# Splitting the first expert of a mixture-of-experts layer: its rows from the last batch get a slot of their own, and gathers go ahead of sums

## The chip, the core and the metric

The kernel runs on one core of a Trainium2 chip. The core has a matrix engine (TensorE, PE in the profile, with its weight loads as PEld), a vector engine (VectorE, DVE), an activation engine (ScalarE, ACT), a general engine (GpSimd, POOL) and a queue that only issues transfers (SyncE, SP). Each engine works through its own list of instructions in order and waits where an input isn't there yet. Transfers issued by SP or POOL run beside them on 16 DMA engines.

The metric is the device time of one execution in microseconds, as the median of several. The profile is that of one such execution.

## The reference

One decoder layer over 16 batches of 256 tokens, width 256, all in float32:

```python
x = ln(x + recurrent(x))                   # gated scan with 16 states
x = ln(x + cross_attention(ctx, x))        # 8 heads of 128; keys: 77 context rows and the 256 tokens
x = ln(x + experts(x))
```

The change is in the last line. `experts` scores every token against 8 experts, keeps the two best with softmax weights, and lets an expert take the first 512 tokens that chose it, in order of the tokens; later ones are dropped:

```python
ones = (weights > 0)
cap_ones = where(cumsum(ones, axis=0) <= expert_capacity, ones, 0)
inter = relu(einsum('ech,eih->eci', tokens, first_linear))     # 256 -> 512
out = einsum('eci,ehi->ech', inter, second_linear) * vals      # 512 -> 256
final = zeros.at[index].add(out)                               # the two experts of a token add up
```

So a token's place in an expert depends on all tokens before it, and the last batch can still bring rows to every expert.

## The kernel before, in words

**Batches.** A loop runs over 16 x 8 pairs of batch and head, `(b, h)`, in the source from L709. For each pair it computes keys and queries (`head_kq`), the softmax, the transposed probabilities and the output, staggered over three pairs. To the pairs hang lists of other steps (`steps`, filled by `at(b, h, f, ...)`): the recurrent part of the next batches, and the last part of the batch before. For batch b-1 these are `project` (heads 2 and 3 of batch b), `turn_tokens` (head 5), `score_experts` and `choose` (head 6), `dispatch` and `settle` (head 7). The last batch has no pairs after it, so its steps follow the loop one after the other (L722 to L728).

**Routing.** `turn_tokens` transposes 256 tokens on PE (px, L532), `score_experts` multiplies by the experts' embeddings (pl, L541), `choose` picks two experts in some twenty small DVE instructions, `dispatch` counts with two small products on PE (pc, L608 and L609) how many tokens each expert already has, which `carry` keeps from batch to batch, and works out for each token the rows it goes to (sidx, L637). Four scatters on POOL (L640, 128 rows of 262 numbers each) then write the tokens into `xg`, a table in DRAM with 512 rows for each expert. Beside its 256 values a row carries the two weights, the token's number, its first expert and its two places. `settle` writes the layer's result for tokens that no expert takes.

**Experts.** After the loop, expert by expert:

- `Rows(e)` loads the 512 rows from `xg` (SP, L747) and works out on DVE from their last columns, in 13 small instructions (L751 to L778), the weight of a row, where the token's other row is (`at`), and where the sum goes (`to`);
- `turn_rows` transposes the rows on PE (L790) and copies them out with DVE (L792) and ACT (L794);
- `first_product` (L803, ReLU on ACT at L810) and `second_product` (L818, scaled on ACT at L825, stored to the table `oe_d` by SP at L828);
- `finish` gathers on POOL, four times 128 rows, what the token's earlier expert gave (L837), adds it and the token on DVE (L850, L852), normalizes (L855 to L859, the power -0.5 on POOL at L129, L863 on DVE), and scatters the finished tokens on POOL (L864). A token with two experts is finished by the later one.

In the source the order is: first product of e, rows and transposes of e+1, second product of e, finish of e, weights of e+2. Weights of expert 0 are loaded two batches before the loop ends.

**What sets the order.** The source only says what depends on what. When the program is built, a planner goes through the instructions with its own estimates of times and puts on each engine what is ready, the earliest in the source first. So an instruction can stand on its engine ahead of others that come before it in the source, and after that the order is fixed: on the chip each engine keeps to it and waits where it must. The planner also waits with a buffer until all uses of what lay there before are over. The buffers of the attention (`work`) are given up as a whole before the expert buffers (`e2`) take their place. In PSUM there are eight banks: two under the tag `mm`, one each under `pk`, `pq`, `pa`, `po`, two under `s`. Before the change the first product uses `mm`, as routing does, and the second one `pa` and `po`.

Of the kernel before, what the change touches and what calls it, by code (L numbers as in the profile page):

```python
# [18 lines left out]
P = 128  # L19
# [19 lines left out]
def decoder_layer(  # L39
# [47 lines left out]
    xg = dram.tile([E * CAP, DX], F32, tag="xg", name="xg")  # L87

    oe_d = dram.tile([E * CAP, D], F32, tag="oe", name="oe")
# [13 lines left out]
    ebase = cpool.tile([P, GT, E], F32, tag="ebase", name="ebase")  # L103
    for e in range(E):
        G.memset(rev[:, :, e : e + 1], float(E - e))
        G.memset(ebase[:, :, e : e + 1], float(e * CAP))
# [54 lines left out]
    w2pool = ctx.enter_context(tc.tile_pool(name="wC", bufs=1))  # L161
    work = ExitStack()
    wpool = work.enter_context(tc.tile_pool(name="wB", bufs=1))
    aw = work.enter_context(tc.tile_pool(name="aw", bufs=1))
    a2 = work.enter_context(tc.tile_pool(name="a2", bufs=2))
# [20 lines left out]
    def load_xT(pr):  # L186

        xTs[pr] = b1.tile([P, DC, PT], F32, tag="xT", name=f"xT{pr}")
        nc.sync.dma_start(xTs[pr], xT[:, pr * PT : (pr + 1) * PT].rearrange("(c p) t -> p c t", p=P))

    def load_x(b):
        xts[b] = xpool.tile([P, 2, D], F32, tag="xt", bufs=3, name=f"xt{b}")
        nc.sync.dma_start(xts[b], x_in[b * S : (b + 1) * S, :].rearrange("(i p) d -> p i d", p=P))
# [61 lines left out]
    def clear(i):  # L255

        xg_z = xg.rearrange("(i p r) d -> i p (r d)", p=P, r=2)
        for j in range(2 * i, 2 * i + 2):
            nc.sync.dma_start(xg_z[j], zero)
# [12 lines left out]
    def rec_in(pr, c):  # L272

        if c == 0:
            hss[pr] = b1.tile([P, NI, PT], F32, tag="hs", name=f"hs{pr}")
# [17 lines left out]
    def rec_state(pr):  # L293
# [5 lines left out]
        dec = b1.tile([NST, PT], F32, tag="dec", name=f"dec{pr}")  # L299
        A.activation(dec, px[0:NST], AF.Exp, bias=xpb[0:NST])  # L300
        A.activation(dec, dec, AF.Exp, scale=-1.0)
        bs = b1.tile([NST, PT], F32, tag="bs", name=f"bs{pr}")
        A.activation(bs, px[32 : 32 + NST], AF.Tanh, bias=xpbh[32 : 32 + NST], scale=0.5)
        zb = b1.tile([NST, PT], F32, tag="zb", name=f"zb{pr}")
# [297 lines left out]
    def dispatch(b):  # L602
# [12 lines left out]
        V.tensor_copy(carry, base[:, GT, :])  # L615
        cum = t3("cum", b)
# [7 lines left out]
        V.tensor_tensor(place, cum, ebase, ALU.add)  # L624
# [13 lines left out]
        for t in range(GT):  # L638
            for c in range(2):
                dma = G.indirect_dma_start(  # L640
                    out=xg[:, :],
                    out_offset=bass.IndirectOffsetOnAxis(ap=sidx[:, t, c : c + 1], axis=0),
                    in_=xs[b][:, t, :],
                    in_offset=None,
                    bounds_check=E * CAP - 1,
                    oob_is_err=False,
                )
                apart("xg", dma)
# [8 lines left out]
    for h in range(H):  # L657
        at(0, h, clear, h)
    for b in range(B):
        nb = b + 1  # L660
        new_pair = nb % PB == 0 and nb < B
        if b > 0:
            at(b, 2, project, b - 1, 0)
            at(b, 3, project, b - 1, 1)
            at(b, 5, turn_tokens, b - 1)
            at(b, 6, score_experts, b - 1)
            at(b, 6, choose, b - 1)
            at(b, 7, dispatch, b - 1)
            at(b, 7, settle, b - 1)
# [38 lines left out]
    heads = [(b, h) for b in range(B) for h in range(H)]  # L708
    for i in range(len(heads) + 2):  # L709
        if i < len(heads):  # L710
            head_kq(*heads[i])
            for f, args in steps[heads[i]]:
                f(*args)
        if i >= 2:
            head_out(*heads[i - 2])
        if i < len(heads):
            head_softmax(*heads[i])
        if 1 <= i <= len(heads):
            head_turn(*heads[i - 1])
        if i == len(heads) - 2 * H:  # L720
            load_expert(0, w2pool)
    project(B - 1, 0)  # L722
    project(B - 1, 1)
    turn_tokens(B - 1)
    score_experts(B - 1)
    choose(B - 1)
    dispatch(B - 1)
    settle(B - 1)  # L728
    work.close()
# [4 lines left out]
    e2 = ctx.enter_context(tc.tile_pool(name="e2", bufs=2))  # L734
    e1 = ctx.enter_context(tc.tile_pool(name="e1", bufs=1))
    es = ctx.enter_context(tc.tile_pool(name="es", bufs=4))
    load_expert(1, e2)

    def narrow(tag, e, dtype=F32):
        return es.tile([P, NS], dtype, tag=tag, name=f"{tag}{e}")  # L740

    class Rows:


        def __init__(self, e):
            self.x = x = e2.tile([P, NS, DX], F32, tag="xe", bufs=3, name=f"xe{e}")
            nc.sync.dma_start(x, xg[e * CAP : (e + 1) * CAP, :].rearrange("(s p) d -> p s d", p=P))  # L747
# [5 lines left out]
            V.scalar_tensor_tensor(dw1, first, float(E - e), dw, ALU.is_equal, ALU.mult)  # L753
# [6 lines left out]
            V.scalar_tensor_tensor(d1, first, float(E - e), d, ALU.is_equal, ALU.mult)  # L760
# [4 lines left out]
            V.scalar_tensor_tensor(gone, other, float(e * CAP) + 0.5, other, ALU.is_lt, ALU.mult)  # L765
# [6 lines left out]
            V.tensor_scalar(late, other, float(e * CAP) + 0.5, float(OOB), ALU.is_gt, ALU.mult)  # L772
# [7 lines left out]
    rows = {0: Rows(0)}  # L780

    xets = {}

    def turn_rows(e):
        x = rows[e].x
        xet = e2.tile([P, DC, CAP], F32, tag="xet", name=f"xet{e}")
        for k in range(DC):
            pt = bank(f"pe{e}_{k}", "pk" if k == 0 else "pq", 1)
            for s in range(NS):
                T.transpose(pt[:, s * P : (s + 1) * P], x[:, s, k * P : (k + 1) * P], ident)  # L790
            if k == 0:
                V.tensor_copy(xet[:, k, :], pt)  # L792
            else:
                A.copy(xet[:, k, :], pt)  # L794
        xets[e] = xet

    def first_product(e):
        xet = xets.pop(e)
        it = e2.tile([P, NF, CAP], F32, tag="it", name=f"it{e}")
        for f in range(NF):  # L800
            pi = bank(f"pi{e}_{f}")
            for k in range(DC):
                T.matmul(  # L803
                    pi,
                    lhsT=w1_s[e][:, k, f * P : (f + 1) * P],
                    rhs=xet[:, k, :],
# [3 lines left out]
            A.activation(it[:, f, :], pi, AF.Relu)  # L810
        return it

    def second_product(e, it):
        y = e2.tile([P, NS, D], F32, tag="ye", name=f"ye{e}")
        for s in range(NS):
            po = bank(f"pf{e}_{s}", "pa" if s % 2 == 0 else "po", 1)
            for f in range(NF):
# [3 lines left out]
                    rhs=w2_s[e][:, f, :],  # L821
# [4 lines left out]
            if s % 2 == 1 and e + 1 < E:  # L826
                r0 = e * CAP + (s - 1) * P
                nc.sync.dma_start(oe_d[r0 : r0 + 2 * P, :].rearrange("(i p) d -> p i d", p=P), y[:, s - 1 : s + 1, :])  # L828
        return y

    def finish(e, y):
        R = rows.pop(e)
        g = None
        if e > 0:
            g = e2.tile([P, NS, D], F32, tag="ge", name=f"ge{e}")
            for s in range(NS):
                G.indirect_dma_start(  # L837
                    out=g[:, s, :],
                    out_offset=None,
                    in_=oe_d[0 : e * CAP, :],  # L840
                    in_offset=bass.IndirectOffsetOnAxis(ap=R.at[:, s : s + 1], axis=0),
                )
# [3 lines left out]
        for a, z in [(0, 2), (2, 4)] if e + 1 < E else [(0, 2), (2, 3), (3, 4)]:  # L846
# [14 lines left out]
            for s in range(a, z):  # L861
# [10 lines left out]
                apart(f"out{e}", dma)  # L872

    turn_rows(0)
    for e in range(E):
        it = first_product(e)
        if e + 1 < E:
            rows[e + 1] = Rows(e + 1)
            turn_rows(e + 1)
        finish(e, second_product(e, it))  # L880
        if e + 2 < E:
            load_expert(e + 2, e2)
# [50 lines left out]
```

## Time and profile before

| what | us |
|---|---|
| median of three runs | 1240.26 (1239.01 to 1243.56) |
| profiled execution, its own time | 1242.35 |
| span of its instructions | 1240.7 |
| busy: PE / DVE / ACT / POOL | 1178.6 / 720.4 / 487.3 / 269.7 |
| mean granted clock of PE | 0.978 of full speed |
| moved by DMA | 59.74 MB |

PE is busy for 95% of the span. This says little about the end of the program, where batches turn into experts; there one has to look at stretches. The lines shown below come from four views. The table by stretches gives busy times of the engines. The timeline has one instruction, or several equal ones, in a line: start, duration, engine, line of the source, operation, output and inputs by name, sizes, count, and in brackets how long the engine had been idle and what ended that. SPq is SP's queue, and its line is the issue of a transfer, not its end. A time given as idle "<-issue" is one for which the profile shows no cause.

### The profile page before, as it was taken

The page shows a single profiled execution, that of the slowest core. Times are in us where ns is not written, and L with a number is a line of the kernel's source. Part 1 is how long each engine was busy: PE and PEld are TensorE (multiplying, and loading weights), DVE is VectorE, ACT ScalarE, POOL GpSimd, SP SyncE. Part 2 cuts the span into 40 slices and gives each one's busy share as a digit, 9 for nine tenths or more (in the row PEclk, how much of TensorE's full clock was granted, in tenths as well). Part 3 has the DMA queues.
Part 4 walks back from the last instruction along what each step waited for, and adds up shares of the span by engine and source line. Part 5 has one row for each costly group of instructions (what it writes and reads, how often), then busy time and mean ns, then how long its engine had stood idle before and what let it go on. Part 6 is the DMA issues. An engine that isn't in the chain of part 4 may idle for free.

```text
span 1240.7 us, 15148 instructions
## 1 busy us (share of the span) xinstructions
PE 1178.6 (95%) x4964; PEld 836.8 (67%) x4964; DVE 720.4 (58%) x2094; ACT 487.3 (39%) x1263; POOL 269.7 (22%) x495
## 2 busy tenths in 40 slices
PE   7799999999999999999999999999999999759993
PEld 3356777677776777677767776777677777636662
DVE  6535654675568455855585547664866454525554
ACT  3134434453344343534453435343534344213331
POOL 3300021122112211131113111211112111216655
PEclk9899999999999999999999999999999999869997
DMA  8630100010001000010001000000000000036751
GB/s 271 231 131 0 37 18 28 9 54 17 29 9 50 18 21 9 25 37 8 16 20 37 4 19 21 19 12 19 2 12 12 19 4 9 24 116 151 187 160 61
DMA packets 42737, 59.74 MB, mean 48 GB/s; under 512 B 7769, under 2 KB 30726, under 8 KB 42658
## 3 DMA queue, kind: packets, MB, share of 16 engines
q1 hardware_dynamic: 35986, 49.54, 12.4%
q0 software_dynamic: 5952, 9.21, 3.3%
q8 instruction: 39, 0.64, 0.2%
q14 instruction: 40, 0.33, 0.1%
q10 hardware_dynamic: 720, 0.01, 0.0%
HBM read 36.02 MB, written 29.98 MB: 53 GB/s over the span
## 4 chain that ended last, share of the span: by engine, by line
PE 76%; DVE 9%; issue 6%; POOL 5%; DMA 3%; ACT 1%; POOLq 0%; SPq 0%; DVEq 0%; ACTq 0%
PE po L481 11%; PE pk L430 10%; PE s L445 10%; PE pw L499 9%; PE pq L435 8%; PE pv L410 8%; PE ph L278 5%; PE pa L468 4%; PE pvc L362 3%; PE px L298 2%; PE pb L468 2%; DMA ge<-oe,at 2%; PE pl L541 1%; POOL out L864 1%; POOL re L129 1%
## 5 line engine op out<-in xcount | busy, mean ns | idle before, releaser
L447 DVE TENSOR_REDUCE nm<-s 128x2 f32<-128x666 f32 x128 | 108.4, 847 | 144.9 <-PE s L445 144.7
L481 PE MATMUL po<-ptt,v 128*128 128x256 f32 (+1 forms) x768 | 189.7, 381 | 2.4 <-DVE ptt L470 2.4
L481 PEld LDWEIGHTS po<-ptt,v 128*128 128x128 f32 (+1 forms) x768 | 143.5, 190 | 57.3 <-issue 33.1
L430 PE MATMUL pk<-kvt,wkv_s 128*128 128x333 f32 x512 | 165.1, 444 | 0.0
L445 PE MATMUL s<-kt,qt 128*128 128x333 f32 x512 | 164.4, 442 | 0.0
L489 ACT ACTIVATE ot<-po,bkv_s 128x256 f32<-128x256 f32 x128 | 60.8, 475 | 234.3 <-PE po L481 232.9
L451 ACT ACTIVATE p<-s,nm 128x333 f32<-128x333 f32 x256 | 135.3, 535 | 37.9 <-DVE nm L447 28.7
L435 PE MATMUL pq<-kvt,wq_s 128*128 128x256 f32 x512 | 131.2, 378 | 0.0
L410 PE MATMUL pv<-wkv_s,kvt 128*128 128x512 f32 x256 | 121.6, 599 | 0.0
L445 PEld LDWEIGHTS s<-kt,qt 128*128 128x128 f32 x512 | 96.5, 189 | 31.3 <-ACT qt L437 0.5
L435 PEld LDWEIGHTS pq<-kvt,wq_s 128*128 128x128 f32 x512 | 96.7, 189 | 30.5 <-issue 0.5
L499 PE MATMUL pw<-wo_s,ot 128*128 128x256 f32 x512 | 116.3, 379 | 0.1
L471 ACT COPY ptt<-pb 77x256 f32<-77x256 f32 x128 | 47.1, 368 | 173.0 <-PE pb L468 170.3
L499 PEld LDWEIGHTS pw<-wo_s,ot 128*128 128x128 f32 x512 | 96.9, 190 | 13.6 <-ACT ot L489 0.5
L430 PEld LDWEIGHTS pk<-kvt,wkv_s 128*128 128x128 f32 x512 | 87.6, 191 | 23.0
L456 DVE TENSOR_SCALAR pn<-p,rs 128x333 f32<-128x333 f32 x256 | 93.2, 398 | 4.2
L640 POOL DMA_INDIRECT xg<-xs,sidx x64 | 67.5, 1055 | 100.1 <-DVE sidx L637 85.4
L470 DVE COPY ptt<-pa 128x512 f32<-128x512 f32 x128 | 87.4, 683 | 0.9 <-issue 0.6
L468 PEld LDWEIGHTS pa<-ident,pn 128*128 128x128 f32 x512 | 63.6, 141 | 34.8 <-DVE pn L456 7.1
L510 POOL TENSOR_TENSOR xb<-xs,bo_s 128x256 f32<-128x256 f32 x32 | 21.2, 683 | 283.2 <-DVE yb L512 283.2
L468 PE MATMUL pa<-ident,pn 128*128 128x128 f32 x512 | 78.5, 274 | 2.4 <-DVE pn L456 2.4
L287 DVE SCALAR_TENSOR_TENSOR cv<-hp,cw,cv 128x512 f32<-128x512 f32 x96 | 71.3, 748 | 2.0
(164 smaller groups left out, 1569.0 us busy)
## 6 DMA issues: line engine op xcount, KB each, us to landing
v<-vc SPq DMA_DIRECT2D x16, 308.0 KB
vc<-vc SPq DMA_DIRECT2D x9, 512.0 KB
xg<-zero SPq DMA_DIRECT2D x16, 262.0 KB
xe<-xg SPq DMA_DIRECT2D x8, 524.0 KB
xT<-in_xT SPq DMA_DIRECT2D x8, 512.0 KB
xt<-in_x_in SPq DMA_DIRECT2D x16, 256.0 KB
w<-in_w1T SPq DMA_DIRECT2D x8, 512.0 KB
w<-in_w2T SPq DMA_DIRECT2D x8, 512.0 KB
```

What stands on the lines that cost most here:

```text
L287: V.scalar_tensor_tensor(cv, hp[:, :, k : k + S], cw[:, c, k : k + 1], cv, ALU.mult, ALU.add)
L410: T.matmul(pv, lhsT=kvts[b][:, k, jc * P : (jc + 1) * P], rhs=wkv_s[:, k, INNER + f0 : INNER + f0 + 512], start=(k == 0), stop=(k == DC - 1),)
L430: T.matmul(pk[:, 0:J], lhsT=wkv_s[:, k, f], rhs=kvt[:, k, :], start=(k == 0), stop=(k == DC - 1))
L435: T.matmul(pq[:, 0:S], lhsT=wq_s[:, k, f], rhs=kvt[:, k, 0:S], start=(k == 0), stop=(k == DC - 1))
L445: T.matmul(s[:, ic, 0:J], lhsT=qt[:, ic * P : (ic + 1) * P], rhs=kt, start=True, stop=True)
L447: V.tensor_reduce(nm, s[:, :, 0:J], AX.X, ALU.max, negate=True)
L451: A.activation(p[:, ic, :], s[:, ic, 0:J], AF.Exp, bias=nm[:, ic : ic + 1], accum_out=sm[:, ic : ic + 1])
L456: V.tensor_scalar(pn[:, ic, :], p[:, ic, :], rs[:, ic : ic + 1], None, ALU.mult)
L468: T.transpose(dst[0:jn, c0 : c0 + P], pn[:, ic, j0 : j0 + jn], ident)
L470: V.tensor_copy(ptt[:, 0:2, :], pt01.rearrange("p (j i) -> p j i", j=2))
L481: T.matmul(po[:, 0:S], lhsT=vs[b][0:jn, jc, h * DH : (h + 1) * DH], rhs=ptt[0:jn, jc, :], start=(jc == 0), stop=(jc == 2),)
L499: T.matmul(pws[b][:, i * D : (i + 1) * D], lhsT=ot[:, h, i * P : (i + 1) * P], rhs=wo_s[:, h, :], start=(h == 0), stop=(h == H - 1),)
```

## The change

Expert 0 is split into two slots. Slot 0 holds the rows that the first fifteen batches sent it, slot 1 those of the last batch; slots 2 to 8 are experts 1 to 7. To this end:

- `xg` and `oe_d` get 256 rows more. Expert 0 keeps rows 0 to 511, slot 1 has rows 512 to 767, the other experts follow (`FIRST`). For the last batch `ebase_last` shifts expert 0's places so that they start at row 512 whatever the count.
- Batch 14's steps `turn_tokens` to `dispatch` move one head earlier (`early`), and `Rows(0)` is written ahead of the last pair of the loop. `turn_rows(0)` is written behind the last batch's `settle`.
- The recurrent part's buffers go to the other side of SBUF and are given up two batches before the end of the loop. Expert buffers that slot 0 needs (`e0`, `es`) take their place.
- The first product uses the banks of `s`, `pa` and `po`, the second one those of `mm`. Slot 1 has two tiles of 128 rows where others have four; both products and the transposes of it are half as wide.
- The gathers of slot e+1 are written right behind the second product of slot e, ahead of `finish(e)`. Weights of experts 1 and 2 are loaded together. The final scatters of all slots are declared free of conflicts with each other.

The core of the diff:

```diff
+    FIRST = [0] + [e * CAP + S for e in range(1, E)]
+    xg = dram.tile([E * CAP + S, DX], F32, tag="xg", name="xg")
+    oe_d = dram.tile([E * CAP + S, D], F32, tag="oe", name="oe")
...
+        if b == B - 2:
+            V.tensor_copy(ebase_last, ebase)
+            for t in range(GT):
+                V.tensor_scalar(
+                    ebase_last[:, t, 0:1], carry[:, 0:1], -1.0, float(CAP), ALU.mult, ALU.add
+                )
...
+    at(1, 0, clear, H)
...
         if b > 0:
+            early = int(b == B - 1)
             at(b, 2, project, b - 1, 0)
             at(b, 3, project, b - 1, 1)
-            at(b, 5, turn_tokens, b - 1)
-            at(b, 6, score_experts, b - 1)
-            at(b, 6, choose, b - 1)
-            at(b, 7, dispatch, b - 1)
+            at(b, 5 - early, turn_tokens, b - 1)
+            at(b, 6 - early, score_experts, b - 1)
+            at(b, 6 - early, choose, b - 1)
+            at(b, 7 - early, dispatch, b - 1)
             at(b, 7, settle, b - 1)
...
+    LAST = E
+    SLOTS = [(0, 0, NS), (0, CAP, GT)] + [(e, FIRST[e], NS) for e in range(1, E)]
...
     def first_product(e):
-        it = e2.tile([P, NF, CAP], F32, tag="it", name=f"it{e}")
+        it = e0.tile([P, NF, CAP], F32, tag="it", name=f"it{e}")
         for f in range(NF):
-            pi = bank(f"pi{e}_{f}")
+            if f == 0:
+                two = ps.tile([P, 2, 512], F32, tag="s", bufs=1, name=f"pi{e}")
+            pi = two[:, f, :] if f < 2 else bank(f"pi{e}_{f}", "pa" if f == 2 else "po", 1)
...
-            po = bank(f"pf{e}_{s}", "pa" if s % 2 == 0 else "po", 1)
+            po = bank(f"pf{e}_{s}")
...
+    def gather(e):
+
+        R = rows[e]
+        gs[e] = e2.tile([P, NS, D], F32, tag="ge", name=f"ge{e}")
+        for s in range(R.n):
+            G.indirect_dma_start(
+                out=gs[e][:, s, :],
+                out_offset=None,
+                in_=oe_d[0 : SLOTS[e][1], :],
+                in_offset=bass.IndirectOffsetOnAxis(ap=R.at[:, s : s + 1], axis=0),
+            )
...
-                apart(f"out{e}", dma)
+                apart("out", dma)
...
     for i in range(len(heads) + 2):
+        if i == len(heads) - 2 * H:
+            rec.close()
+            open_early()
+        if i == len(heads) - 1:
+            rows[0] = Rows(0)
...
     dispatch(B - 1)
     settle(B - 1)
+
     turn_rows(0)
+    work.close()
+    e2 = ctx.enter_context(tc.tile_pool(name="e2", bufs=2))
+    load_expert(1, e2)
+    load_expert(2, e2)
+    for e in range(LAST + 1):
         it = first_product(e)
-        if e + 1 < E:
+        if e < LAST:
             rows[e + 1] = Rows(e + 1)
             turn_rows(e + 1)
-        finish(e, second_product(e, it))
-        if e + 2 < E:
-            load_expert(e + 2, e2)
+        y = second_product(e, it)
+        if e < LAST:
+            gather(e + 1)
+        finish(e, y)
+        if 2 <= e < E - 1:
+            load_expert(e + 1, e2)
```

## The prediction

> **What bounds the kernel now.** I read the windows of 10 us first, then the timeline where TensorE (PE) stops, then GpSimd (POOL) alone through the experts, and last the tail. Columns of the windows: stretch, its length, busy us and instructions of PE, weight load, DVE, ACT and POOL, then granted clock, DMA share, GB/s.
>
> ```profile
> 1060.00:1070.00 10.00, 10.00 (x55) 8.57 (x54) 5.92 (x26) 4.20 (x13) 4.03 (x4) 1.00 0.03 7
> 1070.00:1080.00 10.00, 6.13 (x26) 4.34 (x24) 3.02 (x9) 0.47 (x1) 2.50 (x7) 0.87 0.01 2
> 1080.00:1090.00 10.00, 2.88 (x12) 2.71 (x12) 5.02 (x34) 0.20 (x1) 1.55 (x2) 0.50 0.73 232
> 1090.00:1100.00 10.00, 0.48 (x3) 0.51 (x4) 0.51 (x7) 0.00 (x0) 2.92 (x4) 0.50 0.42 118
> 1100.00:1110.00 10.00, 10.00 (x23) 4.80 (x22) 3.48 (x35) 2.38 (x4) 0.00 (x0) 0.76 0.16 52
> ```
>
> PE is full before 1070 and after 1100. Between lies a hole, in which batch 15 is routed step after step:
>
> ```profile
> 1078.29 1.23 PE L532 MATMUL px<-ident,xs 128*128 128x128 f32 x4 [3.25 <-DVE xs L143]
> 1085.72 0.58 PE L608 MATMUL pc<-on,tri 128*128 128x16 f32 x2 [3.55 <-DVE on L599]
> 1092.86 0.98 POOL L640 DMA_INDIRECT xg<-xs,sidx  x1 [0.30 <-issue]
> 1095.03 1.47 SPq L747 DMA_DIRECT2D xe<-xg  x3
> 1099.49 0.17 DVE L751 TENSOR_TENSOR dw<-xe 128x4 f32<-128x4 f32 x1 [10.76 <-DMA xe<-xg]
> 1101.39 8.80 PE L803 MATMUL pi<-xet,w 128*128 128x512 f32 x16
> ```
>
> The last projection ends at 1075.05, rows land at 1099.49: 24.4 us in which PE has 1.23 (px) + 1.88 (pl) + 1.17 (pc) of work, at half clock. The next limit is POOL, here one turn (gathers of one expert to those of the next):
>
> ```profile
> 1157.74 0.99 POOL L837 DMA_INDIRECT ge<-oe,at  x1 [0.30 <-issue]
> 1159.04 1.14 POOL L837 DMA_INDIRECT ge<-oe,at  x1 [0.30 <-issue]
> 1160.47 0.95 POOL L837 DMA_INDIRECT ge<-oe,at  x1 [0.30 <-issue]
> 1161.73 1.16 POOL L837 DMA_INDIRECT ge<-oe,at  x1 [0.30 <-issue]
> 1165.69 0.76 POOL L129 TENSOR_TENSOR re<-ve,nhalf 128x2 f32<-128x2 f32 x1 [2.79 <-DVE ve L859]
> 1170.03 0.72 POOL L129 TENSOR_TENSOR re<-ve,nhalf 128x2 f32<-128x2 f32 x1 [0.49 <-DVE ve L859]
> 1174.12 0.99 POOL L837 DMA_INDIRECT ge<-oe,at  x1 [0.30 <-issue]
> ```
>
> A turn takes 1174.12-1157.74 = 16.38 us; PE starts an expert every 14.65 (1147.64 to 1162.29). So POOL falls behind, and the tail pays: PE's last product ends at 1220.43, and only then POOL gathers for expert 7.
>
> ```profile
> 1220.43 0.47 ACT L825 ACTIVATE ye<-pf,we 128x256 f32<-128x256 f32 x1 [1.25 <-PE pf L818]
> 1223.13 0.99 POOL L837 DMA_INDIRECT ge<-oe,at  x1 [0.30 <-issue]
> 1229.00 0.76 POOL L129 TENSOR_TENSOR re<-ve,nhalf 128x2 f32<-128x2 f32 x1 [1.09 <-DVE ve L859]
> ```
>
> Tail: 1240.7-1220.43 = 20.3 us, of which 11.7 follow the power at 1229.00.
>
> **Step 1, routing batch 14 one head earlier.** No instruction is added; 4 scatters (xg) move with it. In the trace its xs are final at 1042.6 (L143), px ran at 1049.3, its scatters from 1063.53 to 1068.47. One head is 5.9 us there (pk at 1041.8, 47.3, 52.8, 58.8), so px comes near 1044, scatters end near 1062.6, and SP issues the load of expert 0's rows 1.2 us later (as 1093.84 to 1095.03), 1063.8. It lands near 1068.3, taking the 4.46 us of 1095.03 to 1099.49, in which three loads shared the engines. That load is moved past nothing on SP: after 1044.5 SP issues nothing until 1080.46. POOL is idle there. DVE then has the 13 small Rows instructions (1.2 us, 1099.49 to 1100.64), and it is in order: standing ahead of head 7's softmax they hold it until the rows land. From both sides: 0 (DVE sat idle 6.84 us before 1075.07) to 1068.3-1063.85 = 4.5. I take 0, since batch 14's other steps stood well in this loop. Three more DVE instructions (0.5 us), a ninth clear (262 KB in batch 1, DMA nearly idle): 0, hidden under PE's full row.
>
> **Step 2, expert 0 in the hole.** Its work on PE is 8 transposes (0.8), 7.03 (L803 warm), 6.84 (L818): 14.7 us, from rows, weights and banks (pk, pq, s, pa, po) free before 1075. Room is 24.4-4.3 = 20 us. In the source it stands behind the routing, but the order on an engine is a planner's, which pulls ready work ahead: batch 14's output, written in head 7, ran on POOL at 1043.55, in head 4. I take it that it does so here. Routing may then wait behind a matmul pair (0.86) at each of px, pl, pc: up to 2.6 us, against 2.1 won where px, pl, pc run at full clock (half of 4.3): net 0. The worst order, px behind all of expert 0, costs 13.3 (1091.6 for 1078.3). DVE gets one copy more (0.69), which fits into its 0.84 wait for POOL at 1077.
>
> y of expert 0 lies over the attention's buffers and waits for the last output's landing, as the weights did at 1082.75; its first use is near 1086. Its scatters (POOL, 8.2 us) follow batch 15's, after 1093.84, when POOL sat idle 22.6 us: hidden; without that cover they would delay slot 1's gathers by 8.
>
> **Step 3, the extra slot.** Same scatters, so its load still goes at 1095.03, half as large and without xe0 before it: at best 1097.3 (a 256 KB store took 2.3: issued 1080.46, SP's wait for it over at 1082.75), at worst 1099.49. I take 1098.2. With Rows (1.2) and a half copy (0.35) product 1 starts at 1099.8. PE then does: slot 1, 16 x 0.215 + 16 x 0.214 = 6.86; the turn for slot 2, 0.77; slots 2 to 7, 6 x 14.65 = 87.9; slot 8, 7.03 + 6.84 = 13.87. Sum 109.4. Slot 1 and its transposes are new: 7.3 us on the path. It also adds a 256 KB store and POOL work: 2 gathers at 1.28 (nothing joins there, so each fetches row 0), a power with its wait 1.5, 2 scatters 2.34, 6.4 us in all. POOL does this near 1105 to 1114, when it has nothing else but expert 0's leftover, so I cost it at nothing; if expert 0's scatters slip behind it, slot 2's sums start late by up to 6, which the 1.05 us that POOL then gains per turn takes back over six turns.
>
> **The clock.** The row: PE stopped at 1075.05, the clock halved by 1077.5, after 2.4 us, and came back at 1104.8, 5.3 after 1099.49; the first product took 8.80 for 7.03. The Trainium skill (TensorE: Matmul & The Clock Gate, "Part 1: The HAM clock gate") wants an idle window of about 3.4 us to cool and about 3.4 busy to warm. It speaks against the change: expert 0 ends near 1093.5, a second hole of 5 us is left, PE cools again, and the warm-up is paid at 1099.8 as before. By the rule 3.4 x 0.5 = 1.7 is lost, by the row 1.77. I take the row, and 0.7 for stalls such as that from 1130.85 to 1131.38: PE ends at 1099.8+109.4+1.8+0.7 = 1211.7, **8.7 us earlier**.
>
> **Step 4, gathers ahead of sums.** Each slot's four gathers go on POOL past the power and four scatters of the slot before. A turn loses the 2.79 wait: 16.38-2.79 = 13.6 us of POOL, below 14.65, so PE leads. But each gather now asks for a store just issued. [...]the store above took 2.3, the loaded row load 4.5. Queued behind the waiting gather are POOL's power and scatters of the slot before, and DVE's L863 waits for them. Before, 14 us lay between store and gather.
> Take PE's end of a slot as T. Gather first: y at T+0.5, landed T+2.8[...], gathers to T+8, sums' output to T+16.4, which is T'+1.8 of the next slot; no growth from slot to slot. Last slot: DVE sums at T+4.2 at the latest, power at T+4.5, end T+16.2. Power first (planner finds the store not landed): the last power at T-0.8, end T+10.9. Midway, and by no nearer row: **13.5**, against 20.3: 6.8 us.
>
> **Sum.** 1211.7+13.5 = 1225.2 for the span of 1240.7: 15.5 less. The profiled execution took 1242.35, 1.65 around its span and 2.1 over the median of 1240.26; taken off the median: **1224.8**.
>
> **Rivals.** A: as above. PE's end is at best 1206.9 (routing 2.1 sooner, rows 0.9 sooner, a clock that stays full 1.8), at worst 1213.5 (rows 1.3 later, routing 0.5); with tails of 10.9 to 16.2 and less 0.4: 1217 to 1229. Chance 0.62.
> B: the gathers' order changes nothing, POOL keeps its turn. For: POOL's order is the planner's too. Against: the chain waits on ge in each turn. Slot 2 ends at 1124; its power at 1124.2, then 6 turns as 1133.27 to 1229.00 (95.7), then 11.7: 1231.6, less 0.4 for the median: 1231. Chance 0.14.
> C: the planner keeps source order, expert 0 starts after pc (1086.7), and its second product comes behind slot 1's transposes: 1098.2 + 0.4 + 6.84 + 109.4 + 0.7 = 1215.5 (PE is warm by then), + 13.5 = 1229.0: 1228.6 on the median. For: px to pc stand earlier in the source. Chance 0.10.
> D: routing is held behind expert 0's matmuls, by 2 to 13.3 us: 1226 to 1236. Chance 0.09.
> E, slower: POOL as bound. If the wait for the store (w) adds to POOL's 13.6 each turn, and isn't hidden in PE's time, w = 4.5 makes 18.1; the first such gather is at 1109.2+4.5, the seventh 108.6 later, 1222.3, then 13.6 and 11.7: 1247.6. The end is 1216.1 + 7w, so it decides from w = 3.5, and from 4.4 it is slower by over 0.5%. Against: the store goes at PE's time, so a late POOL finds it landed. Chance 0.05.
>
> 0.5% (6.2 us) is about what a measurement of this kernel tells from no change. Below 1234: A, B, C and most of D: faster 0.92. Same, D's end and a mild E: 0.05. Slower 0.03. The range 1218 to 1234 leaves out D's end, E and a little below A.
>
> **What would show it.** Right: L803's first rows before 1085; px, pl, pc at clock 1.00; the rows' load still near 1095; PE's end near 1212; no DVE wait on ge; the tail 11 to 16. Wrong: pc later than 1088, a DVE wait on xe before 1070, POOL waiting over 5 us ahead of L837 in each turn, or turns of over 15 us.

## The result and the profile after

The changed kernel takes 1230.76 us (median of four runs, 1230.44 to 1232.08), the kernel before beside it 1241.54 (four runs, 1239.01 to 1243.56): ratio 0.9916, 95% interval [0.9894, 0.9938]. A second set on another chip gave 0.9896 [0.9871, 0.9921], or 13.3 us. The forecast was 1224.8 with a range of 1218 to 1234: the time lies in the range, but of 15.5 us forecast some 10.8 came. By spans it is 1240.7 to 1230.4, 10.3 us, and 5.2 us of the sum are missing.

The same stretches of 10 us as before, now of the changed kernel (stretch, length, busy us and instructions of PE, weight load, DVE, ACT, POOL, granted clock, DMA share, GB/s):

```profile
1060.00:1070.00 10.00, 7.04 (x34) 5.54 (x32) 3.47 (x18) 4.14 (x13) 2.81 (x3) 1.00 0.25 60
1070.00:1080.00 10.00, 9.37 (x38) 7.77 (x39) 1.56 (x8) 0.84 (x2) 0.00 (x0) 0.83 0.01 2
1080.00:1090.00 10.00, 8.92 (x35) 4.71 (x34) 6.23 (x27) 2.04 (x5) 2.92 (x7) 1.00 0.25 71
1090.00:1100.00 10.00, 9.11 (x40) 6.82 (x38) 5.47 (x27) 2.93 (x6) 4.76 (x5) 1.00 0.59 197
1100.00:1110.00 10.00, 7.51 (x33) 6.23 (x34) 6.58 (x48) 2.49 (x6) 5.89 (x7) 0.83 0.75 199
```

The hole between 1080 and 1100 is filled, at full clock. But before the change PE worked almost without a break until 1075.05, and now it has only 7.04 us in 1060 to 1070, and a clock of 0.83 in the row after. The timeline of the changed kernel shows why:

```profile
1064.63 0.37 SPq L743 DMA_DIRECT2D xe<-xg  x1
...
1065.58 1.46 PE L484 MATMUL po<-ptt,v 128*128 128x256 f32 x6
...
1069.04 0.17 DVE L748 TENSOR_TENSOR dw<-xe 128x4 f32<-128x4 f32 x1 [3.76 <-DMA xe<-xg]
...
1070.18 0.69 DVE L459 TENSOR_SCALAR pn<-p,rs 128x333 f32<-128x333 f32 x2
1070.63 0.84 PE L471 MATMUL pa<-ident,pn 128*128 128x128 f32 x4 [3.59 <-DVE pn L459]
...
1080.73 0.69 DVE L515 TENSOR_TENSOR yb<-pw,xb 128x512 f32<-128x512 f32 x1 [8.52 <-PE pw L502]
```

The same two places of the kernel before:

```profile
1065.60 1.46 PE L481 MATMUL po<-ptt,v 128*128 128x256 f32 x6
...
1075.07 0.69 DVE L512 TENSOR_TENSOR yb<-pw,xb 128x512 f32<-128x512 f32 x1 [6.84 <-PE pw L499]
```

DVE stands 3.76 us at slot 0's first Rows instruction, until the rows have landed. Behind it in DVE's order is the last head's softmax (L459), and PE waits for that (3.59 us). Just ahead of it PE is level in both profiles (po at 1065.58 and 1065.60). Batch 15's output yb starts at 1080.73, where it started at 1075.07. So the hold costs 5.66 us: the wait, and 1.7 us because PE then runs at half clock from 1071.7 to 1075.1, and some 0.4 that were not taken apart.

Then slot 0's work and the routing of batch 15, interleaved on PE, and slot 1's rows:

```profile
1084.41 0.87 PE L535 MATMUL px<-ident,xs 128*128 128x128 f32 x4 [0.35 <-DVE xs L146]
1085.12 1.02 PE L798 MATMUL pi<-xet,w 128*128 128x512 f32 x2
1086.98 3.68 PE L798 MATMUL pi<-xet,w 128*128 128x512 f32 x8
1090.67 0.36 PE L611 MATMUL pc<-on,tri 128*128 128x16 f32 x2
1092.05 7.07 PE L814 MATMUL pf<-w,it 128*128 128x256 f32 x32
1099.55 0.88 SPq L743 DMA_DIRECT2D xe<-xg  x2
1102.28 0.16 DVE L748 TENSOR_TENSOR dw<-xe 128x2 f32<-128x2 f32 x1 [1.37 <-DMA xe<-xg]
1103.52 4.86 PE L798 MATMUL pi<-xet,w 128*128 128x256 f32 x16 [0.18 <-DVE xet L785]
```

From yb to the issue of the rows' load it is 18.8 us (before: 1075.07 to 1095.03, 20.0), with the whole of expert 0 in between. Last, the tail, with ACT's last scaled product (ye) and the end of POOL's order:

```profile
1205.16 0.75 POOL L132 TENSOR_TENSOR re<-ve,nhalf 128x2 f32<-128x2 f32 x1 [1.03 <-DVE ve L859]
...
1210.90 1.03 POOL L864 DMA_INDIRECT out<-oe,to  x1 [0.74 <-DVE oe L863]
1212.23 0.99 POOL L834 DMA_INDIRECT ge<-oe,at  x1 [0.30 <-issue]
...
1216.07 0.95 POOL L834 DMA_INDIRECT ge<-oe,at  x1 [0.30 <-issue]
1216.47 0.47 ACT L821 ACTIVATE ye<-pf,we 128x256 f32<-128x256 f32 x1 [1.25 <-PE pf L814]
1217.32 1.01 POOL L864 DMA_INDIRECT out<-oe,to  x1 [0.30 <-issue]
1218.36 0.73 POOL L132 TENSOR_TENSOR re<-ve,nhalf 128x2 f32<-128x2 f32 x1
```

The last slot's gathers stand ahead of only one scatter of slot 7. For the gathers of slots 3 to 7 POOL's order is still the old one: power, two scatters, power, two scatters of the slot before, then the four gathers. PE's part ends with ye at 1216.47 (before 1220.43), the last slot's first power comes at 1218.36 (before 1229.00), and from there it is 12.0 us to the end (before 11.7). DVE's wait for ge fell from 20.6 to 10.2 us in all.

### The profile page after: what moved, and what is told of

Same layout as the page of the kernel before. It is cut to its first block, busy times and chain, and to the rows that moved or that the text cites. A ratio compares the mean times of both kernels' runs of the same rounds, so it can differ in the third digit from the quotient of the medians.

```text
span 1230.4 us, 15284 instructions
## 1 busy us (share of the span) xinstructions
PE 1187.3 (96%) x5000; PEld 842.3 (68%) x5000; DVE 725.9 (59%) x2122; ACT 489.4 (40%) x1270; POOL 274.5 (22%) x500
## 4 chain that ended last, share of the span: by engine, by line
PE 82%; DVE 7%; POOL 3%; issue 3%; DMA 3%; ACT 1%; POOLq 0%; SPq 0%; DVEq 0%
PE po L484 12%; PE pk L433 10%; PE s L448 10%; PE pw L502 9%; PE pq L438 8%; PE pv L413 8%; PE ph L281 5%; PE pa L471 4%; PE pi L798 3%; PE pvc L365 3%; PE px L301 2%; PE pf L814 2%; PE pb L471 2%; PE pl L544 1%; DMA xe<-xg 1%
## 5 line engine op out<-in xcount | busy, mean ns | idle before, releaser
L459 DVE TENSOR_SCALAR pn<-p,rs 128x333 f32<-128x333 f32 x256 | 93.1, 397 | 4.2
```

The source lines that it names most:

```text
L459: V.tensor_scalar(pn[:, ic, :], p[:, ic, :], rs[:, ic : ic + 1], None, ALU.mult)
```

## The experiments

Two theories on the missing 5.2 us: the hold of DVE ahead of the last head (step 1, taken at nothing), or POOL, whose turn didn't become 13.6 us. The sets ran on different chips, on which the kernel before took 1240.38, 1242.72 and 1242.85 us, so ratios to it are compared, not times. Runs of one version differ by 1.0 to 3.4 us (in two versions by 5 and more), so differences of 2 us between single profiles stand on little.

**Slot 0's Rows instructions behind batch 15's output.** The load stays where it is; the 13 DVE instructions are bound to stand on DVE behind yb.

```diff
             nc.sync.dma_start(x, xg[r0 : r0 + self.n * P, :].rearrange("(s p) d -> p s d", p=P))
+            self.e, self.r0, self.code = e, r0, code
+
+        def work(self):
+            e, r0, code, x = self.e, self.r0, self.code, self.x[:, 0 : self.n, :]
             narrow = lambda tag, e, dtype=F32: es.tile([P, NS], dtype, tag=tag, name=f"{tag}{e}")[:, 0 : self.n]
...
     settle(B - 1)
+    with tc.issue_after(ybs[B - 1].ins):
+        rows[0].work()
     turn_rows(0)
```

> The changed kernel with one edit: the 13 small DVE instructions on slot 0's rows (dw to the row numbers) are bound behind batch 15's sum yb on DVE; the load itself stays where it is. Hold theory (DVE stood 3.76 us in front of dw, with head 7's pn behind it, and this is the 5.3 us by which yb is late): yb back to about 1075.5, batch 15's rows issued near 1094.3, slot 1's first product near 1098.2, time 1225 to 1226. Rival, POOL paces the experts and an earlier start of PE brings nothing: yb early, but the time stays within 1229 to 1231, with POOL's turns unchanged and a longer tail. Rival, the loss lies in the second cool-down of the clock and not in the hold: 1230, yb still near 1080.

Measured: 1227.28 us (1226.19 to 1228.56), ratio 0.9879 [0.9853, 0.9906]. The timeline of this version:

```profile
1074.42 0.69 DVE L515 TENSOR_TENSOR yb<-pw,xb 128x512 f32<-128x512 f32 x1 [6.84 <-PE pw L502]
1075.03 0.15 DVE L752 TENSOR_TENSOR dw<-xe 128x4 f32<-128x4 f32 x1
```

The hold is gone: yb is 6.3 us earlier than in the changed kernel, of which 0.63 were there ahead of the hold (po at 1064.95), and the wait before it is the old 6.84. The last ye comes at 1210.71, 5.76 us earlier. The end came only 3.5 us earlier in the span: the tail grew from 13.9 to 16.2. The time lies between the two numbers, and by the ratios 2.1 to 4.6 us are won, depending on the set of the changed kernel that it is held against. So the hold is shown as PE's loss, and a second limit a few us behind it.

**Batch 14's routing not moved** (`early = 0`, Rows of slot 0 written behind the last head's steps).

```diff
-            early = int(b == B - 1)
+            early = 0
...
-        if i == len(heads) - 1:
-            rows[0] = Rows(0)
         if i < len(heads):
             head_kq(*heads[i])
             for f, args in steps[heads[i]]:
                 f(*args)
+        if i == len(heads) - 1:
+            rows[0] = Rows(0)
```

> The changed kernel with batch 14's routing steps put back to heads 5, 6, 6, 7, and the load of slot 0's rows behind them. Scatters then end near 1068.5 and slot 0's rows land near 1074.2. Hold theory: in the planned order dw now stands behind head 7's softmax and only in front of yb, which is ready at 1075.1, so the hold nearly goes although the rows come 5.5 us later: yb 1075.5 to 1076.5, time 1225 to 1227. Rival, it is the lateness of the rows that counts: 5.5 later than the changed kernel, 1236.

Measured: 1230.36 us (1230.07 to 1232.08), ratio 0.9912 [0.9885, 0.9938], neither number. The rows landed 3.8 us later than in the changed kernel, and the planner's order put two of slot 0's transposes on PE ahead of the last projections:

```profile
1072.91 0.66 PE L783 MATMUL pe<-ident,xe 128*128 128x128 f32 x2 [2.88 <-DMA xe<-xg]
1073.36 5.30 PE L502 MATMUL pw<-wo_s,ot 128*128 128x256 f32 x18
1078.70 0.69 DVE L515 TENSOR_TENSOR yb<-pw,xb 128x512 f32<-128x512 f32 x1 [4.62 <-PE pw L502]
```

The hold has changed its engine: here PE itself waits for rows, with 18 projections queued behind. When the rows come matters only where an instruction that needs them stands ahead of attention work in an engine's order. With the hold in either form, the earlier routing earned nothing.

**Gathers forced ahead.** Each slot's four gathers are written between the halves of the slot before, and the second half's power is bound behind them on POOL.

```diff
-            r = rsqrt(v, n, P, f"e{e}_{a}")
+            if a == 0 or e == LAST:
+                r = rsqrt(v, n, P, f"e{e}_{a}")
+            else:
+                with tc.issue_after(last[e + 1].ins):
+                    r = rsqrt(v, n, P, f"e{e}_{a}")
...
+            if a == 0 and e < LAST:
+                gather(e + 1)
```

> The changed kernel with the gathers of slot e+1 written between the two halves of finish(e), and the second half's power bound behind them on POOL, so that they do stand ahead of sums. Theory (the planner left POOL's order as it was in all slots but the last, so the gathers' part brought little): no DVE wait on ge, a turn of POOL of at most 14.8 us, tail 11 to 12 instead of 14.0, time 1227.5 to 1229. Rival E of the prediction: the wait for the store that has just been issued adds to POOL's turn: turns of 15.5 or more, time 1232 or more.

Measured: 1231.02 us (1230.32 to 1231.31), ratio 0.9912 [0.9886, 0.9938]. POOL's turns fell to 14.9 us (1148.22 to 1163.10), DVE's wait for ge to 1.8 us in all, and the last gathers began at 1207.28 for 1212.23. But the time didn't move, which neither number had: the last ye is at 1215.22, and the end comes 21.7 us after the last slot's gathers begin, for 18.2 in the changed kernel. What was gained ahead of the gathers is paid behind them, where the second power and two scatters of slot 7 now stand. No rival E either: POOL waited for a fresh store once, 1.5 us.

**Gathers back** (the four gathers right ahead of their own slot's sums).

```diff
         y = second_product(e, it)
-        if e < LAST:
-            gather(e + 1)
+        if e > 0:
+            gather(e)
         finish(e, y)
```

> The changed kernel with gather(e) written right ahead of finish(e), as before the change. Planner theory: POOL's order differs only near slots 0, 1 and the last, where the gathers of slot 8 fall behind the last two scatters of slot 7: tail 1 to 3 us longer, time 1231.5 to 1234. Rival, as predicted: the gathers' part is worth 6.8 us, time 1237 to 1238.

Measured: 1234.6 us (1230.6 to 1235.9), ratio 0.9932 [0.9908, 0.9957]: last ye 1215.35, tail 18.9, the last slot's first power at 1222.11, after all of slot 7's scatters. By the ratios the place of the gathers is worth 2.0 to 4.5 us in the changed kernel, by its two sets; the intervals overlap, so neither the size nor the gain itself is certain.

**The gathers alone**, in the kernel before: nothing else changed.

```diff
-        finish(e, second_product(e, it))
+        y = second_product(e, it)
+        if e + 1 < E:
+            gather(e + 1)
+        finish(e, y)
```

> The kernel before with nothing changed but that each expert's four gathers are written ahead of the sums of the expert before. Theory (the planner keeps POOL's order of the kernel before, and only the last expert's gathers move, between the two last scatters of the expert before it): turns of POOL stay above 16 us, last ye within 0.5 us of 1220.4, the tail 2 to 3.5 us shorter than 20.3, time 1237 to 1238.5. Rival 1 (step 4 as predicted: 6.8 us in the tail): 1233.5. Rival 2 (nothing: the order gives its gain only with the extra slot): 1239.5 to 1240.5.

Measured: 1242.87 us (20 runs) against 1242.72 (23 runs), ratio 0.9998 [0.9989, 1.0007]: nothing, a miss of the theory. POOL in this version, at the end:

```profile
1226.76 0.95 POOL L836 DMA_INDIRECT ge<-oe,at  x1 [0.30 <-issue]
1228.01 1.00 POOL L869 DMA_INDIRECT out<-oe,to  x1 [0.30 <-DVE ue L857]
1229.05 0.73 POOL L129 TENSOR_TENSOR re<-ve,nhalf 128x2 f32<-128x2 f32 x1
1231.41 1.23 POOL L869 DMA_INDIRECT out<-oe,to  x1 [1.64 <-DVE ste L860]
```

At the loop's end this profile stands 1.0 us behind that of before (yb at 1076.10). The last gathers are ahead of one scatter, which brings the first power 1.0 us forward against that; the next scatter then waits 1.64 us and takes it back (from the power to the end 12.65 us, before 11.7). The five turns before the last were as long as ever (15.9 to 17.0).

**The extra slot without the overlap**: slot 0's rows are loaded only once batch 15 is routed, the rest of the change stays.

```diff
-        if i == len(heads) - 1:
-            rows[0] = Rows(0)
...
     settle(B - 1)
+    rows[0] = Rows(0)
     turn_rows(0)
```

> The changed kernel, but slot 0's rows are loaded only once batch 15 has been routed, so that expert 0 is worked on no earlier than in the kernel before; extra slot, gathers and the earlier routing of batch 14 stay. Theory (the gain at PE's end is all from expert 0's place in the hole, and the extra slot costs 7.3 us on PE's path by itself): rows land near 1099, last ye near 1220.4 + 7.3 + 1 = 1228.7 where two row loads share the engines, tail 14, span 1242.5, time 1241.5 to 1244. Rival (the extra slot is hidden, since POOL and not PE sets the end after the hole): last ye later but time 1236 to 1239.

Measured: 1250.37 us (1249.04 to 1251.18), ratio 1.0055 [1.0035, 1.0076]: slower than before, and by more than either theory had. Last ye at 1231.05, 2.3 us later than expected (PE stops once for 1.99 us, at 1202.01, for a copy of DVE's), and a tail of 18.45, not 14. Slot 2's gathers begin 9.6 us behind its first product (1125.89 to 1135.53); in the changed kernel 5.4 (1112.55 to 1117.97). So the overlap gives two things: PE's end 14.6 us earlier (1231.05 for 1216.47), and the beginning of slot 2's gathers 17.6 us earlier.

**No extra slot.** Expert 0's rows from the last batch are left out (256 KB of zeros are written early in place of their store), so the time is that of eight slots.

```diff
-    LAST = E
-    SLOTS = [(0, 0, NS), (0, CAP, GT)] + [(e, FIRST[e], NS) for e in range(1, E)]
+    LAST = E - 1
+    SLOTS = [(0, 0, NS)] + [(e, FIRST[e], NS) for e in range(1, E)]
...
```

> The changed kernel without the extra slot: it leaves out expert 0's rows from the last batch (a 256 KB write of zeros early on stands for their store), so its output lacks them, and its time is read as that of the other eight slots. Theory (PE sets the end, step 3's 7.3 us for slot 1 are all on the path): last ye at 1216.5 - 7.1 = 1209.4, the tail 14, time 1223.5 to 1225. Rival (POOL is the second limit here: with PE earlier POOL falls behind and part is given back in the tail): tail over 16, time 1226 to 1228.

Measured: 1224.98 us (1223.4 to 1226.36), ratio 0.9858 [0.9838, 0.9879]; last ye 1208.72, tail 13.0, about as the theory had it. Of the 7.75 us at PE's end 1.13 are a shorter hold (yb at 1079.60) and 0.76 a stall in the changed kernel's profile (below). Some 5.9 us are left for slot 1 and not 7.3: the cold clock now falls on slot 2's first product (8.70 us for 7.13).

**Both single edits together**: Rows behind yb, and the gathers forced.

> The changed kernel with both single edits together: slot 0's Rows instructions stand on DVE behind batch 15's output, and each slot's four gathers stand on POOL ahead of the second power and the second two scatters of the slot before. Theory (the hold of DVE and the order on POOL are two separate losses; the late gathers are what gave back 2.3 us in the tail when the hold alone was taken away): last projection near 1074.4, last ye near 1210.5, tail 13.8 as with the forced gathers, span 1224.3, time 1224 to 1225.5. Rival (POOL itself is the second limit: with PE 5.7 us earlier its own work ends no sooner, whatever the order): DVE's wait for ge over 8 us, tail over 15.5, time 1227 or more, as with the hold alone.

Measured: 1225.93 us (1224.56 to 1226.93), ratio 0.9865 [0.9846, 0.9884], a little above the theory's number and below the rival's; span 1222.8, last ye 1209.35, tail 13.45, as the theory had it. PE's end and POOL's last gathers can now be set side by side, from the profiles (slot 2 is expert 1):

| version | last ye | expert 1's gathers begin | last slot's gathers begin | span | end after ye | end after last gathers |
|---|---|---|---|---|---|---|
| before | 1220.43 | 1124.98 | 1223.13 | 1240.7 | 20.3 | 17.6 |
| changed | 1216.47 | 1117.97 | 1212.23 | 1230.4 | 13.9 | 18.2 |
| Rows behind yb | 1210.71 | 1115.31 | 1208.69 | 1226.9 | 16.2 | 18.2 |
| gathers forced | 1215.22 | 1118.96 | 1207.28 | 1229.0 | 13.8 | 21.7 |
| gathers back | 1215.35 | 1119.15 | 1216.18 | 1234.2 | 18.9 | 18.0 |
| routing not moved | 1215.90 | 1117.37 | 1210.53 | 1228.4 | 12.5 | 17.9 |
| no extra slot | 1208.72 | 1107.54 | 1203.88 | 1221.7 | 13.0 | 17.8 |
| overlap left out | 1231.05 | 1135.53 | 1231.51 | 1249.5 | 18.5 | 18.0 |
| both | 1209.35 | 1114.27 | 1201.35 | 1222.8 | 13.5 | 21.5 |
| both, first banks back (below) | 1208.20 | 1113.80 | 1201.34 | 1222.8 | 14.6 | 21.5 |

In all versions whose order on POOL the planner chose, the end comes 17.6 to 18.2 us after POOL begins the last slot's gathers, wherever PE's end lies. Where the gathers are forced ahead, it comes 21.5 to 21.7 us after them, and again PE's end doesn't fix it (the last two rows). The chain that the profile follows back from the end says the same: in every version here it leaves PE 32 us or more before the end and then runs over POOL, DVE, ACT and transfers. So PE's end decides in none of them. What counts is when POOL begins expert 1's gathers, how long its turns from there to the last slot's are, and what is left behind those. PE comes in through the first of these and, as far as its products are what the turns wait for, the second.

That is why an edit to one of them gives little. Taking the hold away let POOL begin 2.7 us earlier and saved 0.9 in the six turns: 3.5 us, of 5.8 at PE's end. Forcing the gathers let it begin 1.0 later, saved 5.9 and added 3.6 behind: 1.4 us of span. Both together began 3.7 earlier, saved 7.2 and added 3.3: 7.6 us of span, or 5.9 against the changed kernel's profile from the chip of the next runs (1228.7).

**Three versions on top of both**, run beside the changed kernel on one chip. First the accumulator banks: from expert 1 on as in the kernel before.

```diff
...
-            pi = two[:, f, :] if f < 2 else bank(f"pi{e}_{f}", "pa" if f == 2 else "po", 1)
+            if e < 2:
+                pi = two[:, f, :] if f < 2 else bank(f"pi{e}_{f}", "pa" if f == 2 else "po", 1)
+            else:
+                pi = bank(f"pi{e}_{f}")
...
-            po = bank(f"pf{e}_{s}")
+            po = bank(f"pf{e}_{s}") if e < 2 else bank(f"pf{e}_{s}", "pa" if s % 2 == 0 else "po", 1)
```

> The version with both edits (Rows behind batch 15's output, gathers forced ahead), and from expert 1 on the two products write to the accumulator banks that they had in the kernel before. Theory (the 0.15 us per expert that step 3's turn of 14.65 lacked is the first product's bank: 7.18 us against 7.03): turns of PE back from 14.80 to 14.65, last ye 1.0 us earlier than the 1209.35 of the version with both edits, tail the same, span near 1221.8, ratio to before 0.9857. Rival (the bank isn't it, or POOL sets the end): products stay at 7.13 or more, or the tail grows by what PE gains; ratio 0.9865 within 0.0004.

Measured: 1225.6 us (1224.25 to 1226.92), ratio 0.9868 [0.9841, 0.9895]. All but one of the first products from slot 2 on are back at 7.03 us, PE's turns at 14.65, and the last ye comes 1.15 us earlier (1208.20), as the theory had it; the span is the same 1222.8, as the rival had it. The last ye and the last slot's first power, of the version with both edits, then of this one:

```profile
1209.35 0.47 ACT L825 ACTIVATE ye<-pf,we 128x256 f32<-128x256 f32 x1 [1.25 <-PE pf L818]
1211.05 0.76 POOL L132 TENSOR_TENSOR re<-ve,nhalf 128x2 f32<-128x2 f32 x1 [0.69 <-DVE ve L863]
```

```profile
1208.20 0.47 ACT L828 ACTIVATE ye<-pf,we 128x256 f32<-128x256 f32 x1 [1.25 <-PE pf L821]
1211.04 0.76 POOL L132 TENSOR_TENSOR re<-ve,nhalf 128x2 f32<-128x2 f32 x1 [0.69 <-DVE ve L866]
```

POOL's turn in this version, with the DVE instruction that waits in it:

```profile
1160.96 0.95 POOL L841 DMA_INDIRECT ge<-oe,at  x1 [0.30 <-issue]
1161.94 0.73 POOL L132 TENSOR_TENSOR re<-ve,nhalf 128x2 f32<-128x2 f32 x1
1162.71 0.73 DVE L874 TENSOR_SCALAR oe<-ue,mve,re 128x256 f32<-128x256 f32 x2 [2.58 <-POOL re L132]
1163.41 1.06 POOL L875 DMA_INDIRECT out<-oe,to  x1 [0.74 <-DVE oe L874]
1164.77 0.99 POOL L875 DMA_INDIRECT out<-oe,to  x1 [0.30 <-DVE xet L789]
1167.91 0.76 POOL L132 TENSOR_TENSOR re<-ve,nhalf 128x2 f32<-128x2 f32 x1 [2.15 <-DVE ve L866]
1169.40 1.04 POOL L875 DMA_INDIRECT out<-oe,to  x1 [0.74 <-DVE oe L874]
1170.75 0.98 POOL L875 DMA_INDIRECT out<-oe,to  x1 [0.30 <-DVE mve L863]
1172.04 0.99 POOL L841 DMA_INDIRECT ge<-oe,at  x1 [0.30 <-issue]
```

With the gathers forced a turn is 14.9 us from the third on (here 1157.13 to 1172.04), the same in all versions that force them, whether PE's turn is 14.80 or 14.65: POOL waits 2.15 us for ve, which DVE works out only after it has normalized the half that POOL's own power released. This loop through POOL and DVE leaves PE out.

> The version with both edits; slot 0's whole second product stands on PE ahead of slot 1's transposes, and behind it stand five idle products of 128x256 (2.1 us, their result is read by nothing), so that PE's rest until slot 1's rows land is about 1.2 us. Theory (step 3's clock term: the second rest cools the clock and costs about 1.8 us): granted clock 1.00 in all of 1090 to 1110, slot 1's first product 3.7 us and not 5.0, its transposes 0.4, PE's end 1.5 to 2 us earlier, span near 1221.0, ratio 0.985. Rival (the slow product is waiting, not clock, or what PE gains is given back on POOL): first product over 4.5 us, or last ye earlier and the span as before; ratio 0.9865.

The edit of this second version, for slot 0 (`issue_after` again binds the order):

```diff
-            turn_rows(e + 1)
-        y = second_product(e, it)
...
+        if e != 0:
...
+        else:
+            y = second_product(e, it)
+            idle = bank("idle", "po", 1)
+            with tc.issue_after(self_mm[0].ins):
+                for _ in range(5):
+                    mm = T.matmul(idle[:, 0:D], lhsT=ident, rhs=w2_s[0][:, 0, :], start=True, stop=True)
+            with tc.issue_after(mm.ins):
+                turn_rows(1)
```

`self_mm[0]` is the last instruction of the second product.

Measured: 1231.71 us (1229.69 to 1233.13), ratio 0.9913 [0.9885, 0.9941]. It doesn't answer its question, since the order of DVE changed with it:

```profile
1095.44 0.16 DVE L752 TENSOR_TENSOR dw<-xe 128x2 f32<-128x2 f32 x1 [1.79 <-DMA xe<-xg]
...
1099.99 0.17 DVE L752 TENSOR_TENSOR dw<-xe 128x4 f32<-128x4 f32 x1 [2.15 <-DMA xe<-xg]
...
1101.07 6.47 PE L802 MATMUL pi<-xet,w 128*128 128x256 f32 x16 [4.95 <-DVE xet L789]
```

Slot 1's rows are there at 1095.44, but the copy of its transposes now stands on DVE behind the Rows instructions of slot 2, whose rows land at 1099.99. PE waits 4.95 us for it, and the clock cools during that wait. It is the hold of step 1 for the third time, at another place.

The third version has both of these edits.

> Both of the two other edits on the version with both edits: if each is a term of PE's own path they add, and the tail stays near 13.5: last ye 2.5 to 3 us earlier, span near 1220, ratio 0.984. Rival (POOL is the limit from here): turns of PE 14.65 but tail over 15, span 1221.5 or more.

Measured: 1230.15 us (1227.53 to 1230.68), ratio 0.9897 [0.9869, 0.9925], with the same hold (4.45 us at 1100.95); first products 7.03.

The changed kernel itself, beside them:

> The changed kernel as it is, on the same chip as the three versions above, so that the gain of the best of them is compared directly: theory 0.9916 to before, so the versions are 0.6 to 0.8% faster than the change; rival: the chip of the earlier comparison was another one, and here the changed kernel stands at 0.988 or less.

Measured: 1229.52 us (1229.2 to 1230.43), ratio 0.9896 [0.9871, 0.9921]; the rival's 0.988 isn't excluded by the interval. In this profile PE's stall of 0.76 us in slot 3 is absent, and its turns are 14.80 throughout ((1201.01 - 1112.24)/6). On this chip the version with both edits and the old banks takes 3.9 us less than the changed kernel, and no run of the one reaches into those of the other. Both edits, with or without the old banks, are the fastest versions here that compute all of the result.

## Why the prediction was right and wrong

**What bounds PE, step 2 and the landing of step 3: right.** The hole could be filled, at full clock, and routing wasn't held by expert 0: 1.2 us were won there where I had taken 0 between 2.6 lost and 2.1 won. Rivals C and D fall with that (pc at 1090.67 is 9.9 us behind yb, 10.7 before; expert 0 starts ahead of px). Slot 1's rows landed 2.73 us after the issue, forecast 3.17, and its product began 1.24 us later, forecast 1.6. But of the four signs of being wrong that the prediction names three came: pc later than 1088, a DVE wait on xe before 1070, and turns of over 15 us. The time fell into the range although steps 1 and 4 failed.

**Step 1: wrong, and most of the miss.** "I take 0" was the term that failed. The bound from both sides named the mechanism, 13 Rows instructions ahead of head 7's softmax on an engine in order, and the landing was right (forecast 1068.3, seen 1069.04). But I took the end of the range that suited "batch 14's other steps stood well in this loop", though those wait for no load. The other reason, DVE idle for 6.84 us before 1075.07, counted idle time behind the softmax, while the hold falls ahead of it. And the upper end of 4.5 was too low, at 5.66 measured: it left out the 1.7 us of half clock. (The head of 5.9 us in its sum is 5.7 by the four pk times beside it, which changes nothing.) The first experiment shows this step: without the hold PE's end came 5.76 us earlier.

**Step 3, the turn: 1.05 us short.** 14.65 was the turn with the old banks. In the new ones the first product takes 7.18 us for 7.03, seven times; putting the banks back gave 7.03. The term for clock and stalls (1.8 + 0.7) held: slot 1's product took 4.86 us for 3.62, and 0.76 us were a stall.

**Step 4: wrong, and the size right by luck.** The tail is 13.9 us, forecast 13.5. But the turn of 13.6 us that should give it, and with it "so PE leads", never came. The planner kept POOL's old order save for the end; turns average 15.7 us ((1212.23 - 1117.97)/6). Even with the order forced it is 14.9: of the wait for ve, which I took out whole, the gathers' part goes, but 2.15 us for 2.79 stay, now in POOL's and DVE's own loop. What made the tail short was the overlap: slot 2's gathers began 7.0 us earlier (1117.97 for 1124.98) and the six turns from there took 3.9 us less (94.3 for 98.2), of which 3.0 in the last, where the gathers do stand ahead of one scatter. With 0.6 us more behind the last gathers that is the whole gain of 10.3 us in the span. In the old kernel the gathers alone gave nothing.

**The missing 5.2 us of span**, counted as the prediction counts, by PE's end and a tail, are thus 5.66 for the hold, less 1.2 for the routing, less 0.8 for rows and copies, plus 1.05 for the banks and 0.4 for the tail: 5.1. This is a sum of sizes; taking one term away doesn't give it back in full, as the hold and the banks show.

**The rivals.** B gave 1231, nearer to the time than A, and its premise held: POOL kept its turn but for the last, and the end follows POOL. Its own sum has two errors that nearly cancel: slot 2's first power came 2.3 us later (1126.52 for 1124.2; B has no hold either), and from there to the last slot's it took 91.8 us for 95.7. That the order changes nothing is not shown for the changed kernel, where the last turn is shorter. E, the wait for fresh stores, is refuted: with the order forced POOL waited for a store once, 1.5 us (2.4 with both edits).

## What to carry to other kernels

When a load is moved ahead into a full loop, list for each engine which instruction waits for it first and what stands behind that one in the engine's order. Such a hold was never free here: it came on DVE, on PE and again on DVE, and it also cost the clock. Where a planner sets the order, bind the waiting instructions behind the work that they must not hold. And where a loop of other engines ends a few us after the busiest one, cost every edit by when it lets that loop begin and how long it makes its turns, not by the busiest engine's end alone.

## What the runs showed of the hardware

The clock changes at fixed steps, not at a time counted from PE's stop: it fell 2.4 us after the stop before the change, and 4.7 us after it in the changed kernel. In windows of 0.1 us it changes in the changed kernel near 1071.7 (down), 1075.1, 1102.4 (down) and 1105.8, that is 3.4, 27.3 and 3.4 us apart; before near 1077.5 and 1104.8, 27.3 apart; with Rows behind yb near 1077.4, 1080.8, 1097.8 and 1101.2. All these distances are multiples of 3.41. The Trainium skill (TensorE: Matmul & The Clock Gate, "Part 1: The HAM clock gate") says so: a free-running window of 3413 ns. The prediction took it that a window must be idle for this. It needn't be: that from 1068.3 to 1071.7 had PE busy from 1070.63 on, about a third of it, and the clock fell after PE had been back for 1.1 us. Nor need the rest last a whole window: before the change it was 3.25 us (px, after 1075.05), and the clock fell in the middle of it.

Not expected either: a first product of the same 16 instructions takes 0.15 us longer into the new banks (two of its four in one tile over two banks, the others in `pa` and `po`) than into the two `mm` banks in turn. That it is the banks was shown; what in them costs it stays open.
